# Terms by one transpose, layer 0 by pairs of blocks, and a list scheduler that knows product kinds, in a four-layer graph network on one core

## The chip, the cores and the metric

The kernel runs on one core of one Trainium2 chip. Its engines are TensorE (PE: matmuls and transposes), VectorE (DVE), ScalarE (ACT), GpSimd (POOL) and SyncE (SP, which here only issues DMAs); DMAs are also issued from ACT and POOL. The metric is device time in microseconds (us), the median of some runs. "Granted clock" is the share of full TensorE clock that the profile's rows show.

## The reference

For 16 graphs of N = 1024 nodes with D = 256 features and a symmetric 0/1 adjacency with self loops (about 3% ones), four layers are applied, each with a layer norm and relu ahead of it and its result added to x:

```python
h = relu(layernorm(x)); x = x + relu(h @ W_upd + (adj.T @ (h @ W_msg)) / deg + bias)    # layer 0
h = relu(layernorm(x)); x = x + gat1(h, adj)    # 4 heads of 64, leaky slope 0.01, then relu, + h, a norm per head
h = relu(layernorm(x)); x = x + gat2(h, adj)    # 4 heads of 64, slope 0.2, then elu
h = relu(layernorm(x)); x = x + gat3(h, adj)    # 1 head of 256, slope 0.2
# an attention: Wh = h @ W; e[i,j] = leaky(a_src.Wh[i] + a_dst.Wh[j]); softmax over the neighbours j; alpha @ Wh
```

## The kernel before, in words

The attention is used in a factored form. exp(leaky(s_i + d_j)) is exp(d_j) exp(slope s_i) times max(exp((1-slope) s_i), exp(-(1-slope) d_j)), up to a factor that the softmax drops. So for each head a row r = exp((1-slope) s_i) is spread over all 128 partitions, tt = exp(-(1-slope) d_j) is a scalar per partition, and one VectorE instruction makes a block of weights p = max(r, tt) * mask (`masked`, L1054: 128x1024 for layers 1 and 2, 128x256 for layer 3). TensorE multiplies p with the projected features, scaled by exp(d_j), whose extra column exp(d_j) gives the denominators.

The nodes lie in NB = 8 blocks of 128. For each graph:
- `load_x`, `load_adjr` (L864, adjacency columns by blocks, issued by POOL) and `mask_block` load data; `mask_block` loads a row block of the adjacency (L871), squares it to bf16 on ACT (L876) and has it transposed by a DMA (L883) into the mask.
- `norm_t` (every layer): stats on DVE (L905, L912), rstd by two POOL instructions (L917, L918), a shift on DVE (L924), the normed rows hn on ACT (L937), transposes on PE (L950) and a copy to ht on ACT (L956).
- `layer0`: each block is projected (L966), copied as fp32r to hi (L1081), the rounded part is subtracted in PSUM by a matmul with minus the identity (L1088), and the rest is copied to lo (L1097). Each of the eight gathers runs over 8 blocks, hi and lo (L1110, L1113); the last two columns of hi give the degree. ACT takes the degree (L1119), POOL inverts it (L1122, L1123), ACT scales (L1129). The update is four matmul passes (L1137) and the bias as a two-row fp32r matmul of 256 columns (L1140). DVE adds both (L1146) and adds the relu to x (L1153).
- `heads` (layers 1 and 2): `project_all` (L966 and ACT's copy L984), `terms`, then for each of four heads 8 weight blocks (L1054), each followed by a product of 32 matmuls of 64 columns of p and 65 columns of features (L1194, a stationary tile of 128x64), and an epilogue on DVE, ACT and POOL (L1213 to L1332).
- `layer3`: the same with one head, a stationary tile of 128x128 (L1363), and the store of out on SP (L1398).
- `terms` turns the source terms into rows: two groups of four transposes into rows of 4 (or 1) partitions (L1005), an exp on ACT for each group (L1010), a store to DRAM (L1018), then loads that spread a row over all partitions (L1039).

An fp32 matmul appears as two rows in the profile, an fp32r one as one.

The order of all engines' instructions is written by a list scheduler, `Plan`: `do` records each operation with its engine, a cost in us, what it reads and writes, and a priority, which is TensorE's running position in program order plus `RANK[stage][engine]` plus a slack; `SHIFT` sets off the positions of successive graphs. `emit` then always takes the operation that can start earliest by its costs, and by priority among equals. A graph's operations may begin once the first operation of layer 3 of the graph two before is done by the list, so two graphs are in flight for most of the time. A DMA has a fixed `lag` from its issue to its landing, whatever else is being moved. Tiles come from pools with the numbers of buffers in `BUFS`; the PSUM pool `mm` has four banks.

Of the kernel before, what the change touches and what calls it, by code (L numbers as in the profile page):

```python
# [26 lines left out]
SHIFT = 64.5  # L27
# [3 lines left out]
    "load": (-57, -12, 31, -4, -20),  # L31
    "setup": (-11, -73, -123, -184, -81),
    "norm0": (145, -33, -116, 157, 83),
    "split0": (-76, -27, -143, -178, -68),
    "mask": (-26, 45, 20, 88, -18),
    "gather0": (99, -7, 88, 10, 13),
    "norm1": (-71, -5, -82, -24, -28),
    "project1": (17, 39, 4, 11, 39),
    "weights1": (-57, -2, 47, -12, -4),
    "heads1": (-172, -126, -154, -187, -83),  # L40
    "last1": (-121, -247, -219, -176, -156),
    "norm2": (-199, -12, -128, -69, -50),
    "project2": (-145, -175, -221, -103, -183),
    "weights2": (-2, -8, -49, 24, 18),
    "heads2": (21, -16, -35, 64, -14),
    "last2": (74, 30, 80, 28, 44),
    "norm3": (-87, -191, -295, -306, -160),
    "project3": (131, -75, 4, -44, 2),
    "weights3": (-4, 11, 73, 105, -1),
    "last3": (-60, 20, -26, 62, -10),  # L50
# [4 lines left out]
    "mv": 4, "st": 2, "rstd": 4, "shift": 4, "tt": 3, "dg": 2, "rden": 2, "sth": 1, "mh": 2, "rsh": 2,  # L55
# [16 lines left out]
class Plan:  # L72
# [3 lines left out]

    def __init__(self):
        self.ops, self.pos, self.gate, self.stage = [], 0.0, None, None

    def do(self, eng, cost, fn, r=(), w=(), lag=0.0, slack=0.0):  # L80
# [24 lines left out]
        self.ops.append((eng, cost, lag, fn, deps, bufs, self.pos + slack + RANK[self.stage][ENGINES.index(eng)]))  # L105
# [3 lines left out]
    def emit(self):  # L109
# [6 lines left out]
        done, free, held = [None] * n, {}, {}  # L116

# [5 lines left out]
        while ready:  # L123
            best = None
            for k in ready:
                eng, cost, lag, fn, deps, bufs, prio = self.ops[k]
                at = free.get(eng, 0.0)
                for d in deps:
                    same = self.ops[d][0] == eng and not self.ops[d][2]
                    at = max(at, done[d] + (0.0 if same else self.WAIT[self.ops[d][0]]))  # L130
# [13 lines left out]
            eng, cost, lag, fn, deps, bufs, _ = self.ops[k]  # L144
# [5 lines left out]
            free[eng] = at + cost  # L150
            done[k] = at + cost + lag
# [433 lines left out]
def tile_factored(  # L585
# [88 lines left out]
    def fetch(tile, part, out_of, src):  # L674

        do("act", 0.5, lambda: nc.scalar.dma_start(out_of(tile.t), src), w=[(tile, part)], lag=2.5)
# [167 lines left out]
    def load_x(b):  # L844
# [3 lines left out]
        for k in range(0, NB, NB // 2):  # L848
# [7 lines left out]
                lag=4.5,  # L856
# [630 lines left out]
```

## Time and profile before

| | |
|---|---|
| median of 3 runs | 2854.28 us (2850.51 to 2854.32) |
| the profiled execution | 2862.98 us, of which the span is 2861.1 us |
| mean granted TensorE clock | 0.969 |
| busy: PE, PE weight loads, DVE | 2652.2, 2316.5, 2447.7 us |
| busy: ACT, POOL | 1189.9, 721.1 us |
| DMA | 285.24 MB, mean 100 GB/s |

The span runs from the first to the last instruction of one profiled execution; the rest of its time lies around it. Engines work side by side, so busy times don't add up; an engine's idle time costs something only where it lies on the chain of work that ended last. The out stores' last VectorE instruction of each graph shows the graphs' ends: the first graph ends at 425.5 us, the second at 604.6, and from then on one follows another after some 169 us up to 2634.2; the last two end at 2795.3 and 2853.1.

### The profile page before, as it was taken

To read this page: it belongs to the slowest core of one execution; us is meant where nothing else is said; L and a number is where in the kernel's file an instruction comes from. 1 tells how busy PE (TensorE), PEld (TensorE's weight loads), DVE (VectorE), ACT (ScalarE), POOL (GpSimd) and SP (SyncE) were. 2 spreads that over 40 slices of the span, in tenths; PEclk is the share of its full clock that TensorE was granted. 3 is DMA by queue.
4 is the path that set the end of the run, shared out by engine and by line. 5 is a ranking of instruction groups with operands and counts; after the bars stand their busy time and mean duration, and the time that the engine had idled before them with its cause. 6 is when DMAs were issued, how large, how long until landed. Compare 5 with 4: busy or idle time off the path is not lost.

```text
span 2861.1 us, 93412 instructions
## 1 busy us (share of the span) xinstructions
PE 2652.2 (93%) x41131; PEld 2316.5 (81%) x41131; DVE 2447.7 (86%) x5014; ACT 1189.9 (42%) x2881; POOL 721.1 (25%) x811
## 2 busy tenths in 40 slices
PE   6977998999999999999999999999999999999786
PEld 5767886888888888888888888888888888888675
DVE  2579887898998988989898998989899898989984
ACT  4342525344343534535353444535344353443222
POOL 2321311323231222313123231222323122231100
PEclk9989999999999999999999999999999999999898
DMA  9612244542524345253533624353262435424010
GB/s 236 143 38 83 51 89 125 124 115 53 163 70 108 109 106 134 53 126 93 122 109 68 150 67 115 110 122 106 68 154 69 101 109 128 112 53 106 31 42 28
DMA packets 346153, 285.24 MB, mean 100 GB/s; under 512 B 145525, under 2 KB 310778, under 8 KB 345738
## 3 DMA queue, kind: packets, MB, share of 16 engines
q1 hardware_dynamic: 209424, 209.83, 26.7%
q0 software_dynamic: 133152, 67.12, 12.9%
q8 instruction: 324, 5.31, 0.8%
q10 hardware_dynamic: 3162, 2.24, 0.3%
q14 instruction: 91, 0.75, 0.1%
HBM read 228.21 MB, written 17.37 MB: 86 GB/s over the span
## 4 chain that ended last, share of the span: by engine, by line
PE 75%; DVE 15%; DMA 3%; POOL 2%; ACT 2%; issue 2%; SPq 0%; ACTq 0%; DVEq 0%; POOLq 0%
PE acc L1194 28%; PE acc L1363 15%; PE mm L966 13%; DVE p L1054 7%; PE mm L1110 4%; PE mm L1137 4%; PE mm L1113 4%; PE mm L950 4%; DVE st L905 2%; DMA mask<-sq 1%; POOL rstd L918 1%; PE mm L1140 1%; DVE x L1332 1%; PE mm L1005 1%; PE mm L1088 1%
## 5 line engine op out<-in xcount | busy, mean ns | idle before, releaser
L1054 DVE SCALAR_TENSOR_TENSOR p<-r,tt,mask 128x1024 f32<-128x1024 f32 (+1 forms) x1536 | 1468.6, 1012 | 65.7 <-PE acc L1363 44.0
L1194 PEld LDWEIGHTS acc<-wide,p 128*64 128x64 f32 x32768 | 1005.8, 140 | 168.4 <-issue 84.8
L1194 PE MATMUL acc<-wide,p 128*64 128x65 f32 x32768 | 1061.8, 225 | 78.9 <-DVE p L1054 48.5
L966 PE MATMUL mm<-f_w,ht 128*128 128x264 f32 (+2 forms) x2048 | 532.6, 403 | 5.0 <-ACT wide L984 2.5
L1363 PE MATMUL acc<-wide,p 128*128 128x257 f32 x2048 | 474.2, 386 | 12.2 <-DVE p L1054 12.2
L1363 PEld LDWEIGHTS acc<-wide,p 128*128 128x128 f32 x2048 | 382.5, 191 | 71.7 <-issue 11.2
L966 PEld LDWEIGHTS mm<-f_w,ht 128*128 128x128 f32 x2048 | 382.6, 198 | 69.3 <-ACT ht L956 6.4
L937 ACT ACTIVATE hn<-x,shift,rstd 128x256 f32<-128x256 f32 x512 | 273.1, 595 | 149.7 <-DVE shift L924 126.5
L876 ACT ACTIVATE sq<-nat 128x1024 bf16<-128x1024 int32 x128 | 136.0, 1062 | 322.2 <-DMA mask<-sq 293.5
L1110 PE MATMUL mm<-wide,adjr 128*128 128x258 f32 x1024 | 258.9, 292 | 1.6 <-ACT f_deg L1119 1.6
L1113 PE MATMUL mm<-wide,adjr 128*128 128x256 f32 x1024 | 251.8, 285 | 2.7 <-ACT wide L1097 2.7
L950 PE MATMUL mm<-f_ident,hn 128*128 128x128 f32 x1024 | 170.7, 300 | 79.9 <-ACT hn L937 78.9
L1284 ACT ACTIVATE t<-t,mh,rsh 128x64 f32<-128x64 f32 x512 | 176.9, 430 | 160.4 <-DVE mh L1274 160.3
L984 ACT COPY wide<-mm 128x264 f32<-128x264 f32 (+1 forms) x384 | 139.7, 378 | 248.9 <-PE mm L966 247.6
L917 POOL TENSOR_SCALAR rstd<-mv 128x4 f32<-128x4 f32 x128 | 60.6, 473 | 652.7 <-DVE mv L912 630.8
L950 PEld LDWEIGHTS mm<-f_ident,hn 128*128 128x128 f32 x1024 | 123.0, 150 | 114.1 <-ACT hn L937 96.1
L1110 PEld LDWEIGHTS mm<-wide,adjr 128*128 128x128 f32 x1024 | 197.7, 193 | 8.4 <-ACT f_deg L1119 1.8
L1122 POOL TENSOR_SCALAR dg<-f_deg 128x1 f32<-128x1 f32 x128 | 54.4, 425 | 588.6 <-ACT f_deg L1119 586.8
L956 ACT COPY ht<-mm 128x512 f32<-128x512 f32 x256 | 144.9, 580 | 138.9 <-PE mm L950 138.0
L1113 PEld LDWEIGHTS mm<-wide,adjr 128*128 128x128 f32 x1024 | 196.3, 192 | 3.0 <-ACT wide L1097 2.9
L1267 POOL TENSOR_SCALAR rsh<-mh 128x8 f32<-128x8 f32 x64 | 51.5, 805 | 554.1 <-DVE mh L1262 551.9
L905 DVE BATCH_NORM_STATS2 st<-x 128x6 f32<-128x256 f32 x512 | 186.0, 415 | 3.8 <-DMA x<-in_x_dram 1.9
(100 smaller groups left out, 2390.9 us busy)
## 6 DMA issues: line engine op xcount, KB each, us to landing
r<-rd SPq DMA_DIRECT2D x144, 512.0 KB
nat<-in_adj_dram SPq DMA_DIRECT2D x128, 512.0 KB
adjr<-in_adj_dram POOLq DMA_DIRECT2D x128, 512.0 KB, 5.0
out_dram<-o SPq DMA_DIRECT2D x128, 128.0 KB
x<-in_x_dram SPq DMA_DIRECT2D x31, 512.0 KB
mask<-sq SPq DMA_TRANSPOSE x128
p<-in_L_gnn_W_dram ACTq DMA_DIRECT2D x2, 256.0 KB
x<-in_x_dram ACTq DMA_DIRECT2D x1, 512.0 KB
```

Of the source, the lines that this page charges most:

```text
L905: lambda st=st, ib=ib, k=k: nc.vector.bn_stats(st.t[:, k, :], xs.t[:, ib, :]),
L937: nc.scalar.activation(hn.t[:, k, :], xs.t[:, hf * nh + q, :], AF.Relu, bias=shift.t[:, q : q + 1], scale=rstd.t[:, q : q + 1],)
L950: nc.tensor.transpose(pt.t[:, k, c, :], hn.t[:, k, c * P : (c + 1) * P], ident)
L956: nc.scalar.copy(ht.t[:, :, i0 : i0 + 2 * P].rearrange("p c (k i) -> p k c i", k=2), pt.t)
L966: nc.tensor.matmul(ps.t[:, : hi - lo], ht.t[:, c, ib * P : (ib + 1) * P], w.t[:, c, lo:hi], start=(c == 0), stop=(c == KC - 1),)
L984: lambda ib=ib, ps=ps: nc.scalar.copy(wh.t[:, ib, :cols], ps.t[:, :cols]),
L1054: lambda: nc.vector.scalar_tensor_tensor(w.t[:, : hi - lo], r.t[:, lo:hi], tt.t[:, jb, h : h + 1], mask.t[:, jb, lo:hi], op0=ALU.max, op1= ...
L1110: nc.tensor.matmul(ps.t[:, : D + 2], a.t[:, ib, :], hi.t[:, ib, : D + 2], start=(ib == 0), stop=False)
L1113: nc.tensor.matmul(ps.t[:, :D], a.t[:, ib, :], lo.t[:, ib, :D], start=False, stop=(ib == NB - 1))
L1194: nc.tensor.matmul(ps.t[c : c + 64, g, q * E1 : (q + 1) * E1], p.t[:, i2 * 64 : (i2 + 1) * 64], xw.t[:, jb, h * E1 : (h + 1) * E1], start= ...
L1284: nc.scalar.activation(t.t[:, ib, :], t.t[:, ib, :], AF.Identity, bias=mb.t[:, 3, ib : ib + 1], scale=rs.t[:, ib : ib + 1],)
L1363: nc.tensor.matmul(ps.t[:, q, : D + 1], w.t[:, q * P : (q + 1) * P], wh.t[:, jb, : D + 1], start=(jb == 0), stop=(jb == NB - 1),)
```

## The change

- `terms`: exp is taken first, on ACT, of all eight blocks' source columns (8 x 4 or 8 x 1) into a small tile es; one transpose turns it into 32 (or 8) rows of 128; ACT copies them out, and the store to DRAM writes 32 (or 8) rows of 512 bytes.
- `layer0`, split: two blocks are projected into one PSUM bank; each of the two copies and the subtraction takes both, 512 columns.
- `layer0`, update: both blocks of a pair share a bank. The bias comes first, as one two-row matmul of 512 columns, then the eight weight passes. DVE's two operations take 512 columns. The gathers, the degree and its inverse stay by block.
- `layer3`: out is stored by pairs of blocks.
- The list: each product has a kind (c: a 64-column product of layers 1 and 2, r: fp32r, f: all others; an update begins as r and ends as f), and `EMPTY` adds a cost where the kind changes. Each large DMA has a transfer time `dma`; transfers follow one another on one clock, `moved`, and an issue is not placed earlier than some 2 us before that clock comes free. Some costs of operations are new.
- All of `RANK`, `SHIFT` and the slack of the epilogues of heads 0 to 2 have new numbers.

The core of the diff (three of the twenty rows of `RANK`; other loads get `dma` in the same way as the two shown):

```diff
-SHIFT = 64.5
+SHIFT = 59.5
...
 RANK = {
-    "norm0": (145, -33, -116, 157, 83),
+    "norm0": (-17, -86, -77, -102, -43),
...
-    "heads1": (-172, -126, -154, -187, -83),
+    "heads1": (38, 4, 67, -106, 2),
...
-    "norm3": (-87, -191, -295, -306, -160),
+    "norm3": (102, -18, -111, 50, -13),
...
+    EMPTY = {"cf": 0.12, "cr": 0.12, "fc": 0.09, "fr": 0.09, "rc": 0.09, "rf": 0.19}
+
+    AHEAD = 2.0
...
-    def do(self, eng, cost, fn, r=(), w=(), lag=0.0, slack=0.0):
+    def do(self, eng, cost, fn, r=(), w=(), lag=0.0, slack=0.0, kind="f", dma=0.0):
...
+                eng, cost, lag, fn, deps, bufs, prio, kind, dma = self.ops[k]
                 at = free.get(eng, 0.0)
+                if eng == "pe":
+                    at += self.EMPTY.get(kept + kind[0], 0.0)
+                if dma:
+                    at = max(at, moved - self.AHEAD - cost)
...
-            free[eng] = at + cost
-            done[k] = at + cost + lag
+            free[eng] = done[k] = at + cost
+            if eng == "pe":
+                kept = kind[-1]
+            if dma:
+                moved = done[k] = max(moved, done[k]) + dma
+            done[k] += lag
...
-        do("pool", 1.0, lambda: nc.gpsimd.dma_start(a.t, src), w=[a], lag=6.0)
+        do("pool", 1.0, lambda: nc.gpsimd.dma_start(a.t, src), w=[a], lag=2.0, dma=2.9)
...
-        do("sp", 0.1, lambda: nc.sync.dma_start(nat.t, adj[b, ib * P : (ib + 1) * P, :]), w=[nat], lag=4.5)
+        do("sp", 0.1, lambda: nc.sync.dma_start(nat.t, adj[b, ib * P : (ib + 1) * P, :]), w=[nat], lag=2.0, dma=2.2)
...
-    def project(ps, ht, ib, w, lo, hi):
+    def project(ps, ht, ib, w, lo, hi, k=0):
 
 
         def go():
+            out = ps.t[:, : hi - lo] if hi - lo > D else ps.t[:, k, :]
             for c in range(KC):
                 nc.tensor.matmul(
-                    ps.t[:, : hi - lo],
+                    out,
                     ht.t[:, c, ib * P : (ib + 1) * P],
                     w.t[:, c, lo:hi],
-                    start=(c == 0),
+                    start=(c == 0 and k == 0),
                     stop=(c == KC - 1),
+                    skip_group_check=k > 0,
                 )
 
         do("pe", 0.88, go, r=[(ht, ib // 2), w], w=[ps])
...
-        for g in range(2):
-            pt = buf(mm_p, "mm", [P, 4, P])
-
-            def turn(pt=pt, g=g):
-                for q in range(4):
-                    nc.tensor.transpose(pt.t[:nh, q, :], wh.t[:, 4 * g + q, scol : scol + nh], ident)
-
-            do("pe", 0.46, turn, r=[(wh, 4 * g + q) for q in range(4)], w=[pt])
-
-            def raise_r(pt=pt, g=g):
-                nc.scalar.activation(
-                    r4.t[:nh, g * 512 : (g + 1) * 512],
-                    pt.t[:nh].rearrange("p q i -> p (q i)"),
-                    AF.Exp,
-                    scale=1.0 - slope,
-                )
-
-            do("act", 0.6, raise_r, r=[pt], w=[(r4, g)])
-        do("sp", 0.1, lambda: nc.sync.dma_start(rd.t, r4.t[:nh, :]), r=[r4], w=[rd], lag=2.2)
+        m = NB * nh
+        es = buf(small, "es", [P, nh, NB])
+        do(
+            "act",
+            0.25,
+            lambda: nc.scalar.activation(
+                es.t, wh.t[:, :, scol : scol + nh].rearrange("p n h -> p h n"), AF.Exp, scale=1.0 - slope
+            ),
+            r=[(wh, ib) for ib in range(NB)],
+            w=[es],
+        )
+        pt = buf(mm_p, "mm", [P, 512])
+        do(
+            "pe",
+            0.11,
+            lambda: nc.tensor.transpose(pt.t[:m, :P], es.t.rearrange("p h n -> p (h n)"), ident),
+            r=[es],
+            w=[pt],
+        )
+        do("act", 0.25, lambda: nc.scalar.copy(r4.t[:m, :P], pt.t[:m, :P]), r=[pt], w=[r4])
+        do(
+            "sp",
+            0.1,
+            lambda: nc.sync.dma_start(rd.t.rearrange("h (n i) -> (h n) i", n=NB), r4.t[:m, :P]),
+            r=[r4],
+            w=[rd],
+            lag=2.2,
+        )
 
...
-        for ib in range(NB):
-            ps = buf(mm_p, "mm", [P, 512])
-            project(ps, ht, ib, w0, 0, D)
+        for n in range(0, NB, 2):
+            ps = buf(mm_p, "mm", [P, 2, D])
+            for k in range(2):
+                project(ps, ht, n + k, w0, 0, D, k)
+            parts = [n, n + 1]
             do(
                 "act",
-                0.27,
-                lambda ib=ib, ps=ps: nc.scalar.copy(hi.t[:, ib, :D], ps.t[:, :D]),
+                0.48,
+                lambda n=n, ps=ps: nc.scalar.copy(hi.t[:, n : n + 2, :D], ps.t),
                 r=[ps],
-                w=[(hi, ib)],
+                w=[(hi, ib) for ib in parts],
             )
             do(
                 "pe",
-                0.13,
-                lambda ib=ib, ps=ps: nc.tensor.matmul(
-                    ps.t[:, :D], minus, hi.t[:, ib, :D], start=False, stop=True, skip_group_check=True
+                0.23,
+                lambda n=n, ps=ps: nc.tensor.matmul(
+                    ps.t, minus, hi.t[:, n : n + 2, :D], start=False, stop=True, skip_group_check=True
                 ),
-                r=[(hi, ib)],
+                r=[(hi, ib) for ib in parts],
                 w=[ps],
+                kind="r",
             )
             do(
                 "act",
-                0.27,
-                lambda ib=ib, ps=ps: nc.scalar.copy(lo.t[:, ib, :D], ps.t[:, :D]),
+                0.48,
+                lambda n=n, ps=ps: nc.scalar.copy(lo.t[:, n : n + 2, :D], ps.t),
                 r=[ps],
-                w=[(lo, ib)],
-            )
-            mask_block(b, ib, mask)
+                w=[(lo, ib) for ib in parts],
+            )
+            for ib in parts:
+                mask_block(b, ib, mask)
...
-            do("pe", 1.92, gather, r=[adjr[jb], hi, lo], w=[ps])
+            do("pe", 1.9, gather, r=[adjr[jb], hi, lo], w=[ps], kind="r")
             dg = buf(small, "dg", [P, 1])
-            o = buf(work, "o", [P, D])
+            pair_of = jb % 2
+            if not pair_of:
+                o = buf(work, "o", [P, 2, D])
...
-                0.35,
-                lambda ps=ps, dg=dg, o=o: nc.scalar.activation(o.t, ps.t[:, :D], AF.Copy, scale=dg.t),
+                0.38,
+                lambda ps=ps, dg=dg, o=o, q=pair_of: nc.scalar.activation(o.t[:, q, :], ps.t[:, :D], AF.Copy, scale=dg.t),
                 r=[ps, dg],
-                w=[o],
-            )
-            pu = buf(mm_p, "mm", [P, 512])
-
-            def update(pu=pu, jb=jb):
-                for c in range(KC):
-                    nc.tensor.matmul(
-                        pu.t[:, :D], ht.t[:, c, jb * P : (jb + 1) * P], w0.t[:, c, D:], start=(c == 0), stop=False
-                    )
-                nc.tensor.matmul(pu.t[:, :D], pair.to_broadcast([2, P]), b0.t, start=False, stop=True)
-
-            do("pe", 1.0, update, r=[(ht, jb // 2), (dg, "in"), w0, b0], w=[pu])
+                w=[(o, pair_of)],
+            )
+            if not pair_of:
+                continue
+            pu = buf(mm_p, "mm", [P, 2, D])
+
+            def update(pu=pu, j0=jb - 1):
+                nc.tensor.matmul(
+                    pu.t,
+                    pair.to_broadcast([2, P]),
+                    b0.t.rearrange("k (o d) -> k o d", o=1).to_broadcast([2, 2, D]),
+                    start=True,
+                    stop=False,
+                )
+                for q in range(2):
+                    for c in range(KC):
+                        nc.tensor.matmul(
+                            pu.t[:, q, :],
+                            ht.t[:, c, (j0 + q) * P : (j0 + q + 1) * P],
+                            w0.t[:, c, D:],
+                            start=False,
+                            stop=(q == 1 and c == KC - 1),
+                        )
+
+            do("pe", 2.17, update, r=[(ht, jb // 2), (dg, "in"), w0, b0], w=[pu], kind="rf")
             do(
                 "dve",
-                0.45,
-                lambda pu=pu, o=o: nc.vector.tensor_tensor(o.t, o.t, pu.t[:, :D], op=ALU.add),
+                0.63,
+                lambda pu=pu, o=o: nc.vector.tensor_tensor(o.t, o.t, pu.t, op=ALU.add),
                 r=[pu],
                 w=[o],
             )
             do(
                 "dve",
-                0.35,
+                0.62,
                 lambda o=o, jb=jb: nc.vector.scalar_tensor_tensor(
-                    xs.t[:, jb, :], o.t, 0.0, xs.t[:, jb, :], op0=ALU.max, op1=ALU.add
+                    xs.t[:, jb - 1 : jb + 1, :], o.t, 0.0, xs.t[:, jb - 1 : jb + 1, :], op0=ALU.max, op1=ALU.add
                 ),
                 r=[o],
-                w=[(xs, jb)],
+                w=[(xs, jb - 1), (xs, jb)],
...
-                do("pe", 0.96, product, r=[p, xw], w=[ps])
+                do("pe", 0.94, product, r=[p, xw], w=[ps], kind="c")
...
-            epilogue(b, h, ps, wh, xs, 19.0 if h + 1 < H else 0.0)
+            epilogue(b, h, ps, wh, xs, 13.0 if h + 1 < H else 0.0)
...
+            o = buf(work, "o", [P, 2, D])
             for q in range(2):
-                ib = 2 * i2 + q
-                o = buf(work, "o", [P, D])
                 do(
                     "dve",
                     0.42,
-                    lambda q=q, ib=ib, ps=ps, o=o, k=k: nc.vector.scalar_tensor_tensor(
-                        o.t, ps.t[:, q, :D], rdn[:, k + q : k + q + 1], xs.t[:, ib, :], op0=ALU.mult, op1=ALU.add
+                    lambda q=q, i2=i2, ps=ps, o=o, k=k: nc.vector.scalar_tensor_tensor(
+                        o.t[:, q, :],
+                        ps.t[:, q, :D],
+                        rdn[:, k + q : k + q + 1],
+                        xs.t[:, 2 * i2 + q, :],
+                        op0=ALU.mult,
+                        op1=ALU.add,
                     ),
                     r=[ps, xs],
-                    w=[o],
+                    w=[(o, q)],
                 )
-                do(
-                    "sp",
-                    0.1,
-                    lambda ib=ib, o=o: nc.sync.dma_start(out[b, ib * P : (ib + 1) * P, :], o.t),
-                    r=[o],
-                    lag=3.0,
-                )
+            do(
+                "sp",
+                0.1,
+                lambda i2=i2, o=o: nc.sync.dma_start(
+                    out[b, i2 * 2 * P : (i2 + 1) * 2 * P, :].rearrange("(q p) d -> p q d", p=P), o.t
+                ),
+                r=[o],
+                lag=2.0,
+                dma=1.2,
+            )
```

## The prediction

> **What bounds the kernel now.** I read the page first, then the groups by line, then TensorE (PE) alone: its busy time between the second and the fourteenth graph's end, its timeline in one graph, its waits.
>
> ```profile
> span 2861.1 us, 93412 instructions
> ...
> PE 2652.2 (93%) x41131; PEld 2316.5 (81%) x41131; DVE 2447.7 (86%) x5014; ACT 1189.9 (42%) x2881; POOL 721.1 (25%) x811
> ...
> PE 75%; DVE 15%; DMA 3%; POOL 2%; ACT 2%; issue 2%; SPq 0%; ACTq 0%; DVEq 0%; POOLq 0%
> ...
> 604.00:2634.00 2030.00, 1957.16 (x30838) 1710.56 (x30834) 1828.73 (x3735) 892.45 (x2160) 548.62 (x598) 0.98 0.42 104
> ```
>
> The fourth line is the window from 604 to 2634 us, in which twelve graphs end: 169.2 us for each, with PE busy 163.1 and VectorE (DVE) 152.4. PE is idle 6 us a graph, and the chain that ends last lies 75% on it. So what is saved on PE there is saved in time, until DVE, 11 us lower, stops it.
>
> PE rows overlap (a matmul's row includes its pipeline), so I cost by the distance from start to start, in a timeline of PE:
>
> ```profile
> 1009.86 1.02 PE L1137 MATMUL mm<-f_w,ht 128*128 128x256 f32 x4
> 1010.81 0.38 PE L1140 MATMUL mm<-f_bias,f_pair 2*128 2x256 f32 x1
> 1011.12 3.02 PE L1194 MATMUL acc<-wide,p 128*64 128x65 f32 x96
> 1014.07 1.13 PE L1137 MATMUL mm<-f_w,ht 128*128 128x256 f32 x4
> ...
> 1048.65 0.60 PE L1005 MATMUL mm<-f_ident,wide 128*4 128x128 f32 x4
> 1049.08 1.03 PE L1363 MATMUL acc<-wide,p 128*128 128x257 f32 x4
> ...
> 1090.29 7.69 PE L1194 MATMUL acc<-wide,p 128*64 128x65 f32 x256
> 1097.90 1.13 PE L1137 MATMUL mm<-f_w,ht 128*128 128x256 f32 x4
> ```
>
> The update of one block with its bias takes 1011.12 - 1009.86 = 1.26 us. Four weight passes, 0.216 apart inside a run, are 0.86 of it; so the bias matmul (L1140, two rows, 256 columns) costs 0.40. A fp32r matmul of that width costs 0.118 in the gather (L1110 to L1113, start to start); the other 0.28 is change: 0.09 before it, 0.19 behind it. A 64-column product of layer 1 or 2 (32 matmuls) costs (1097.90 - 1090.29)/8, less one change at the end, 0.94. The way from such a product to any other costs 0.12 before the first other matmul and 0.10 at it (the L1137 row is 1.13 behind L1194, 1.02 behind the gather); the way back costs 0.09. Four turns of the terms cost 0.43.
>
> The one regular stall, in windows:
>
> ```profile
> 1117.00:1118.30 1.30, 1.26 (x10) 0.68 (x8) 1.30 (x8) 0.82 (x2) 0.03 (x1) 1.00 1.09 407
> 1118.30:1122.80 4.50, 0.01 (x1) 0.01 (x1) 4.20 (x19) 1.70 (x6) 3.43 (x5) 0.94 0.50 190
> 1122.80:1126.00 3.20, 3.20 (x11) 2.22 (x12) 3.20 (x15) 3.20 (x7) 2.14 (x3) 0.50 0.98 236
> 1126.00:1130.00 4.00, 4.00 (x14) 3.22 (x14) 4.00 (x8) 2.04 (x6) 2.23 (x2) 0.61 1.05 305
> ...
> PE mm L950 <- ACT hn L937: 54.0, 12, 4.5
> ```
>
> Once a graph PE waits 4.5 us for the norm of layer 3, while the other graph in flight is between its terms and its weights. The clock column shows 0.50 and 0.61 for the 7.2 us behind it: 3.2x0.50 + 4.0x0.39 = 3.2 us more. The stall costs 7.7 us.
>
> **The change part by part**, for all 16 graphs.
>
> *Terms.* Eight transposes become one, 48 times: 48 x 7 x 0.109 = 36.6 us off PE. All eight blocks must now be projected first; then exp of 32 columns on ScalarE (ACT; 0.25, as L1029), the transpose, and a copy of 128 columns (between L1119 with 0.16 and L1081 with 0.38), in place of two exps of 0.58. In the trace the last projection copy ends near 1117.8 and the rd store is issued at 1118.95; the new chain is 0.25 + 0.27 + 0.27 with three handovers, the same within 0.2. DVE's first weight waits for r until 1126, and has stats to do meanwhile; without that cover it is 0.2 x 48 = 10 us either way. I take 0. The store now leaves from 32 rows of 512 B: no row is near; between no difference and another r wait like the four there are (13.0 us in all). I take 0. SP issues one store as before.
>
> *Update and bias.* Before: 128 bias matmuls x 0.40 = 51 us, and 57 of the updates (counted in the trace) follow a 64-column product: 57 x 0.22 = 12.5. After: 64 updates; the bias of 512 columns stands first: 0.236 (twice 0.118) + 0.19 behind it = 0.43, 27 us; its entry is 0.22 for some 28 and 0.09 for 36, 9.4; half the returns to a product, no longer in the bias's 0.19, 22 x 0.09 = 2. Saved 63.5 - 38.6 = 25. What the trace lacks is the step from a 64-column product or a gather straight into the two-row tile. The Trainium skill, "TensorEngine Tiling (Array Packing)", Key Properties, says that a change of tiling mode drains the array. The rows agree for two rows and for 64 columns, and show none between fp32 and fp32r of one tile (four L966 and an L1088 take 0.98 = 0.86 + 0.118). By this rule the entry from a gather, which had cost nothing into L1137, now costs 0.09, and I have counted it. Bounds: entry nothing, 34 saved; entry 0.3 each, 15. The same rule speaks against the new list: EMPTY charges 0.09 and 0.19 for fp32 to fp32r and back, which only the two-row tile pays, and too little into other work (0.12, where the rows show 0.22). It will hold apart kinds that mix freely.
>
> *Split.* 8 passes and a 512-column subtraction per pair take what two blocks took (1.73 + 0.24). The subtractions cut into products less often: 41 entries x 0.22 and 30 returns x 0.14, halved, 6.6. I take 5 (2 to 7). ACT copies 512 columns (0.58, as L956) for 2 x 0.376, so lo of a pair is there some 1 us later than that of its first block was; products of the other graph lie over it. Without them: 64 x 1 us.
>
> *DVE.* Add and relu-add of a pair at about 0.69 each (L1214 and L1246, 512 columns) for 2 x 0.42 each: 64 x 0.31 = 20 us of busy time off, 1.2 a graph. Off the path mostly; 0.
>
> *Stores of out.* 128 of 128 KB become 64 of 256 KB, each waiting for the second o (0.48 later). Behind them on SP are x and nat loads, and nobody of PE waits for those in the middle; at the very end 0.5 us. 0.
>
> *The list.* The trace has 333 ways from products to other work and 259 ways back without a bias: 333 x 0.22 + 259 x 0.09 = 97 us. The parts above dealt with 57 and 41 of the ways out, 22 us. Of the other 75, a list that sees a cost on changes keeps more work together; but DVE makes a weight in 1.28 us and PE uses it in 0.94, so PE must leave often. Bounds: 0 and half, 37; I take a fifth, 15. Pacing DMAs moves nat, adjr, x, r and out issues on SP, ACT and POOL's queues: in the middle covered (DMA share 0.42); in the first 100 us (share 1.07 in its window, PE busy 73) from -10 to +15; 0. All ranks, SHIFT and the epilogue's slack are new: where the 7.7 us stall falls next is not in the trace. I take it as it is.
>
> Sum on PE: 36.6 + 25 + 5 + 15 = 82. In the chain of that window PE's lines sum to 84%:
>
> ```profile
> by line: PE acc L1194 32.8%; PE acc L1363 16.9%; PE mm L966 14.1%; PE mm L1110 5.0%; PE mm L1137 4.6%; PE mm L1113 4.5%; PE mm L950 4.1%; DVE p L1054 3.0%; DVE st L905 1.9%; issue 1.8%; PE mm L1140 1.5%; POOL rstd L918 1.4%; DVE x L1332 1.1
> ```
>
> So 69 us. The profiled execution took 2862.98 (2861.1 of span and 1.9 around it), 8.7 over the median of the three runs; 2863 - 69 = 2794, and against the median 2854.3 - 69 = **2785**.
>
> **Rivals.**
> 1. *The stall goes.* A better matched order gives PE work under the norm of layer 3. "TensorE: Matmul & The Clock Gate", Part 1, says that an idle window of about 3.4 us halves the clock; the windows above agree (4.5 us of idle, then 0.50), and no shorter stall here shows where it begins. By the row alone half the stall is worth half of 7.7; by the rule it is worth 2.3 + 3.2 = 5.5. Some 14 graphs x 5.5 to 7.7 = 77 to 108 more: 2677 to 2708, and about 2750 if a third of the graphs gain. For it: the list that made this order reckoned updates at 1.0 where 1.26 are taken. Against: the stall is a chain of DVE, POOL and ACT (stats, pow, hn), and less PE work leaves less to lay over it. 18%.
> 2. *DVE becomes the bound.* If its 16.8 us of idle a graph stay, a graph takes 151.2 + 16.8 = 168.0: 1.2 x 16 = 19 us, 2835. Against: of 174 us of its named waits in the window some 130 are for PE or PE's copies. 12%, 2815 to 2845.
> 3. *Slower: a second stall.* Longer runs of one kind keep PE from the other graph's norm or first products, and the idle passes the point where the clock halves. Price 7.7 a graph against 69/16 = 4.3 gained: one more such stall in over 56% of the graphs turns the sign; in all of them 16 x 3.4 = 54 slower, 2908; likeliest some 2870. 6%.
> 4. *The list does not matter and the savings fall into waits*: no change, 4%.
>
> The first reading has 60%: 2750 to 2815.
>
> **How the numbers follow.** A difference under 0.2%, some 6 us, is no change for this kernel. Faster: 60 + 18 + 12 = 90%; same 4; slower 6. The range takes in the first reading with its bounds (36.6 + 15 + 2 up to 36.6 + 34 + 7 + 37, times 0.84: 45 to 96), the nearer half of the stall's case and most of DVE's: 2715 to 2832.
>
> **What would show it.** One L1005 transpose per term and 48 in all; L1140 with 512 columns, 64 times, some 0.43 to its next start; PE busy in a middle graph near 158 for 163.1, DVE near 151; fewer ways out of L1194 than 333; the L950 wait for hn still once a graph at 4 to 5 us with a clock of 0.5 behind it. It is wrong if that wait is gone or doubled, if PE's idle in the middle grows past 10 us a graph, or if the first 425 us, which graph 0 takes now, move by over 20.

## The result, and the profile after

The changed kernel takes 2807.62 us (median of 4 runs, 2803.09 to 2812.79) against 2854.3 before: a ratio of 0.9838 [0.9817, 0.986], 47 us less. That lies within the range. The way to it is another than the forecast's.

The span and the busy times of the page:

```profile
span 2807.9 us, 92058 instructions
...
PE 2535.0 (90%) x40667; PEld 2288.6 (82%) x40667; DVE 2422.9 (86%) x4886; ACT 1158.5 (41%) x2753; POOL 652.4 (23%) x811
```

PE works 117 us less (2652.2 to 2535.0), not 82, and yet the span is only 53 us shorter (the profiled execution of before was 8.7 over its median; by medians it is 47). DVE works 25 us less.

To see where 117 us became 47, each kernel is cut at the ends of the second and the fourteenth graph, into the front, the middle (twelve graphs) and the tail. The columns of a window are: its stretch and length, busy time (and number) of PE, its weight loads, DVE, ACT and POOL, the granted clock, the DMA share, GB/s. First before:

```profile
0.00:604.60 604.60, 522.69 (x7801) 456.14 (x7803) 452.63 (x942) 238.90 (x581) 152.83 (x193) 0.95 0.48 109
604.60:2634.20 2029.60, 1956.76 (x30822) 1710.16 (x30820) 1828.34 (x3735) 892.45 (x2160) 548.62 (x598) 0.98 0.42 104
2634.20:2861.10 226.90, 172.80 (x2520) 150.17 (x2516) 166.77 (x341) 58.57 (x140) 19.66 (x20) 0.90 0.11 36
```

and after:

```profile
0.00:547.40 547.40, 477.34 (x7099) 422.58 (x7099) 422.13 (x883) 224.14 (x535) 143.04 (x191) 0.95 0.51 117
547.40:2562.20 2014.80, 1865.34 (x30490) 1694.84 (x30492) 1809.70 (x3637) 869.37 (x2062) 488.08 (x601) 0.97 0.44 105
2562.20:2807.90 245.70, 192.34 (x3086) 171.17 (x3082) 191.11 (x368) 65.03 (x158) 21.29 (x21) 0.88 0.10 34
```

Front and tail have to be taken together, because the new order does less of later graphs ahead of the second end, and more behind the fourteenth. In us:

| | PE busy | PE idle | length |
|---|---|---|---|
| middle | 1956.8 to 1865.3 (-91) | 72.8 to 149.5 (+77) | 2029.6 to 2014.8 (-15) |
| front and tail | 695.5 to 669.7 (-26) | 136.0 to 123.4 (-13) | 831.5 to 793.1 (-38) |

So the two ends grew shorter by all that PE saved there, and by some idle time as well. In the middle five sixths of the saving turned into idle time of PE: a graph takes 167.9 us for 169.1, with PE busy 155.4 for 163.1, and idle 12.5 for 6.1. The waits of PE, all of them, then the first two of DVE, in the middle of after (us in total, times, longest):

```profile
PE acc L1241 <- DVE shift L940: 108.6, 12, 9.2
PE acc L1241 <- issue: 27.8, 23, 4.2
PE acc L1410 <- DVE p L1082: 7.9, 12, 0.7
PE acc L1241 <- DVE p L1082: 4.3, 10, 0.5
```

```profile
DVE f_mx L1049 <- ACT wide L1002: 94.6, 27, 7.3
DVE rden L1260 <- PE acc L1241: 33.8, 34, 5.3
```

And DVE's first line in the middle of before:

```profile
DVE f_mx L1022 <- ACT wide L984: 55.3, 12, 4.7
```

PE's wait for hn, the regular one of before, is gone from after's middle. PE now waits 9 us once a graph for DVE, in one piece; DVE waits up to 7.3 us for a projection that PE has not yet made (wide is ACT's copy of it, f_mx the maximum that DVE takes of it for the terms). They wait for each other by turns. Before, PE's one regular wait was 4.5 us, and this one of DVE's 4.6. One of PE's waits, in its timeline (start, length, line, tiles, count, and the idle time before with what ended it):

```profile
1059.69 6.17 PE L983 MATMUL mm<-f_w,ht 128*128 128x264 f32 x27
1065.79 13.29 PE L1241 MATMUL acc<-wide,p 128*64 128x65 f32 x448
1079.01 0.28 PE L1033 MATMUL mm<-f_ident,es 128*32 128x128 f32 x1
1088.31 3.56 PE L1241 MATMUL acc<-wide,p 128*64 128x65 f32 x64 [9.03 <-DVE shift L940]
```

and DVE's timeline over the same time:

```profile
1077.40 0.69 DVE L1371 SCALAR_TENSOR_TENSOR y<-y,t 128x512 f32<-128x512 f32 x1
1078.12 0.69 DVE L1379 TENSOR_TENSOR x<-x,y 128x512 f32<-128x512 f32 x1
1078.73 1.22 DVE L1222 TENSOR_TENSOR wide<-wide 128x1024 f32<-128x1024 f32 x1
...
1082.96 0.69 DVE L1379 TENSOR_TENSOR x<-x,y 128x512 f32<-128x512 f32 x1
1083.69 1.41 DVE L921 BATCH_NORM_STATS2 st<-x 128x6 f32<-128x256 f32 x4
1085.01 0.36 DVE L928 BATCH_NORM_AGGREGATE mv<-st 128x2 f32<-128x6 f32 x4
1085.29 1.37 DVE L921 BATCH_NORM_STATS2 st<-x 128x6 f32<-128x256 f32 x4
1086.58 0.36 DVE L928 BATCH_NORM_AGGREGATE mv<-st 128x2 f32<-128x6 f32 x4
1086.88 1.28 DVE L1082 SCALAR_TENSOR_TENSOR p<-r,tt,mask 128x1024 f32<-128x1024 f32 x1
```

PE has used up 14 weights in one run of 448 matmuls, and its projections lie before that run. DVE then has 9 us without a weight in it: the end of layer 2 for one graph, the statistics of its layer 3, the scaling of features for the other. The weight that PE needs is made at 1086.88 (the wait carries the name of L940, the instruction behind it). The windows:

```profile
1079.20:1088.30 9.10, 0.09 (x1) 0.02 (x1) 8.86 (x27) 1.54 (x4) 2.67 (x4) 0.62 0.68 240
1088.30:1092.00 3.70, 3.69 (x66) 3.63 (x67) 3.70 (x5) 2.05 (x4) 2.93 (x2) 0.56 1.21 269
1092.00:1096.00 4.00, 4.00 (x116) 3.83 (x117) 4.00 (x4) 3.04 (x6) 0.00 (x0) 1.00 0.77 136
```

DVE is busy 8.86 of the 9.10 us: PE waits for an engine that is at work. The clock of 0.56 behind it costs 3.7 x 0.44 = 1.6, so by its lines the stall takes 10.7 us a graph, for 7.7 before. What it is worth in time is another question (v1_tuned below).

The single products are what they were costed at. In PE's timeline:

```profile
848.85 0.27 PE L1033 MATMUL mm<-f_ident,es 128*32 128x128 f32 x1
848.96 10.57 PE L1410 MATMUL acc<-wide,p 128*128 128x257 f32 x48
859.45 0.49 PE L1172 MATMUL mm<-f_bias,f_pair 2*128 2x512 f32 x1
859.87 1.99 PE L1181 MATMUL mm<-f_w,ht 128*128 128x256 f32 x8
...
1001.04 0.28 PE L1145 MATMUL mm<-wide,adjr 128*128 128x256 f32 x1
1001.25 0.50 PE L1172 MATMUL mm<-f_bias,f_pair 2*128 2x512 f32 x1
1001.67 1.99 PE L1181 MATMUL mm<-f_w,ht 128*128 128x256 f32 x8
```

The transpose takes 0.11 from start to start, the bias 0.42, and the way from a gather into the bias 0.21, which is 0.118 and 0.09 of change.

### The profile page after: what moved, and what is told of

Its sections match the earlier page's. It is cut to its first block, busy times and chain, and to the rows that moved or that the text cites. A ratio compares the mean times of both kernels' runs of the same rounds, so it can differ in the third digit from the quotient of the medians.

```text
span 2807.9 us, 92058 instructions
## 1 busy us (share of the span) xinstructions
PE 2535.0 (90%) x40667; PEld 2288.6 (82%) x40667; DVE 2422.9 (86%) x4886; ACT 1158.5 (41%) x2753; POOL 652.4 (23%) x811
## 5 line engine op out<-in xcount | busy, mean ns | idle before, releaser
L1241 PE MATMUL acc<-wide,p 128*64 128x65 f32 x32768 | 1052.9, 227 | 204.3 <-DVE shift L940 117.6
L983 PE MATMUL mm<-f_w,ht 128*128 128x264 f32 (+2 forms) x2048 | 481.6, 390 | 4.4 <-ACT ht L972 3.9
L1410 PEld LDWEIGHTS acc<-wide,p 128*128 128x128 f32 x2048 | 388.9, 192 | 84.2 <-DVE p L1082 13.8
L966 PE MATMUL mm<-f_ident,hn 128*128 128x128 f32 x1024 | 153.8, 291 | 26.6 <-ACT hn L953 25.1
L934 POOL TENSOR_TENSOR rstd<-rstd,f_mhalf 128x4 f32<-128x4 f32 x128 | 164.8, 1287 | 10.7
L879 POOL DMA_DIRECT2D adjr<-in_adj_dram x128 | 120.9, 944 | 164.8 <-PE mm L1145 159.1
```

The lines of the kernel that those rows point to most:

```text
L934: nc.gpsimd.tensor_tensor(rstd.t, rstd.t, mhalf[:, :nh], op=ALU.pow)
L966: nc.tensor.transpose(pt.t[:, k, c, :], hn.t[:, k, c * P : (c + 1) * P], ident)
L983: nc.tensor.matmul(out, ht.t[:, c, ib * P : (ib + 1) * P], w.t[:, c, lo:hi], start=(c == 0 and k == 0), stop=(c == KC - 1), skip_group_che ...
L1241: nc.tensor.matmul(ps.t[c : c + 64, g, q * E1 : (q + 1) * E1], p.t[:, i2 * 64 : (i2 + 1) * 64], xw.t[:, jb, h * E1 : (h + 1) * E1], start= ...
L1410: nc.tensor.matmul(ps.t[:, q, : D + 1], w.t[:, q * P : (q + 1) * P], wh.t[:, jb, : D + 1], start=(jb == 0), stop=(jb == NB - 1),)
```

## The experiments

Each kernel was run beside before; ratios are against before of the same runs. Where a kernel is compared with after, the two ratios are subtracted and taken of 2854 us; as either has an interval of about 0.002 on each side, such a difference is good to some 9 us, and a share worked out from it to 0.2 or 0.3.

### The terms' transpose earlier (e8_turn_moved)

In after the transpose stands 12.4 us behind its exp in this layer. Here the order of after is kept, and only the transpose, its copy, the rd store and the first spread are moved up to where their inputs are ready.

```diff
+        new = dict(when)
+        for k in self.turns:
+            t = when[k - 1][0] + self.ops[k - 1][1] + 0.2
+            for q, step in ((k, 0.4), (k + 1, 0.45), (k + 2, 2.4), (k + 5, 0.0)):
+                new[q] = min(new[q], (t, 0))
+                t = new[q][0] + step
```

> The changed kernel's list, but once it is made, four steps of each of the 48 terms (transpose on PE, ACT's copy, the rd store, the first spread of r) are taken out and put where their inputs are ready; all other instructions keep their order. Theory A (the 9.0 us wait of PE once a graph comes from the terms' transpose standing behind some 13 products of the other graph in PE's queue, so that r lands 12 us late): the wait falls to 0 to 5 us, PE's idle in the middle from 12.5 to 5 to 8 us a graph, granted clock in the middle back from 0.970 to 0.98 or more, time 2715 to 2760. Rival B (the wait is the norm chain of layer 3 on DVE, POOL and ACT, as in the kernel before, and r is not what is late): the wait stays at 8 to 9 us and the time within 10 us of 2808.

2828.42 us, 0.9913 [0.9895, 0.993]: 21 us slower than after (the rival had the wait right and the time too low), and the wait is still 8.5 us (102.1 us for 12 in the middle). PE is not held by a late r: r came early, and DVE, whose order is fixed, was busy with other work, 8.57 us of one such wait of 8.80. That theory fell. Why the time grew is open; PE's waits in the middle for which the profile names no cause (issue) rose from 27.8 to 46.2 us. This run cannot say whether the list put that other work there because it reckoned with a late r; v1_tuned bears on that.

### No cost on changes of kind (e1_no_kinds)

```diff
-    EMPTY = {"cf": 0.12, "cr": 0.12, "fc": 0.09, "fr": 0.09, "rc": 0.09, "rf": 0.19}
+    EMPTY = {}
```

> The changed kernel with EMPTY empty: a change of kind costs the list nothing. The ranks were chosen with the charges, so the order as a whole suits it less and the time may be anywhere from 2780 to 2950. What is tested is PE's count of ways from a 64-column product to other work, 163 in the changed kernel and 333 before. Theory A (the charges keep kinds together): 260 or more ways, and PE busy 25 to 45 us over the 2535 of the changed kernel. Rival B (ranks and pairs brought the count down): under 200 ways, PE busy within 15 us of 2535.

3038.69 us, 1.0644 [1.062, 1.0667]. Ways out of 64-column products: 245, for 163 in after and 333 in before; PE is busy 2620.5. PE's longest waits:

```profile
PE acc L1241 <- DVE p L1082: 140.0, 65, 6.2
PE mm L966 <- ACT hn L953: 110.5, 12, 25.8
PE acc L1241 <- DVE wide L1224: 65.0, 6, 10.8
```

The costs do hold kinds together (82 ways out fewer), under these ranks. But without them PE is busy 85 us more and the time is 230 us longer, more than either theory had, since the list went another way at many places, into waits of up to 25.8 us. The 85 us are not the price of the ways: 82 of them at 0.22 out and 0.09 back are some 25, and part of the rest is a lower granted clock (0.94 in the middle, for 0.97). RANK was chosen with the costs, so this is no price of the costs alone; that stays open.

### No transfer clock (e3_no_clock)

```diff
-        do("pool", 1.0, lambda: nc.gpsimd.dma_start(a.t, src), w=[a], lag=2.0, dma=2.9)
+        do("pool", 1.0, lambda: nc.gpsimd.dma_start(a.t, src), w=[a], lag=6.0)
...
-        do("sp", 0.1, lambda: nc.sync.dma_start(nat.t, adj[b, ib * P : (ib + 1) * P, :]), w=[nat], lag=2.0, dma=2.2)
+        do("sp", 0.1, lambda: nc.sync.dma_start(nat.t, adj[b, ib * P : (ib + 1) * P, :]), w=[nat], lag=4.5)
```

> The changed kernel without the clock of transfers: each DMA has its old fixed lag. Same ranks. Graph 1 ends at 547 us in the changed kernel and at 605 before. Theory A (the front's gain is the paced DMA order): the end of graph 1 goes back by 30 us or more, to 577 or later, and the rest stays within 2%. Rival B (the front's gain is the ranks' and less PE work): the end of graph 1 stays within 15 us of 547.

2937.36 us, 1.0296 [1.0269, 1.0324]. Its windows over the first 100 us and to the end of the second graph, then after's first 100 us:

```profile
0.00:100.00 100.00, 65.84 (x358) 55.88 (x359) 20.68 (x81) 43.59 (x91) 26.60 (x56) 0.97 1.12 228
0.00:604.40 604.40, 482.59 (x7099) 424.94 (x7099) 424.34 (x885) 222.46 (x532) 135.92 (x192) 0.93 0.46 106
```

```profile
0.00:100.00 100.00, 82.59 (x476) 69.57 (x478) 30.55 (x110) 51.15 (x116) 36.09 (x71) 0.98 1.09 217
```

The front holds the same 7099 matmuls as after's and ends 57 us later; 52 of these are idle time of PE (121.8 for 70.1). The DMA engines moved no more in after's first 100 us (217 GB/s for 228). PE's waits for a transfer in the front, first of e3, then of after:

```profile
PE mm L725 <- DMA p<-in_L_gnn_W_dram: 15.6, 3, 14.3
PE mm L1139 <- DMA adjr<-in_adj_dram: 9.0, 3, 4.2
```

```profile
PE mm L1142 <- DMA adjr<-in_adj_dram: 3.1, 2, 2.6
```

So 22 of the 52 us are transfers that came later for PE. Another 27 are longer waits for DVE's weights and epilogues (p and t), since the list made another order of everything. The middle was to stay within 2% and became 3.4% longer. For these ranks the clock is worth the whole gain of the front. Against before, whose ranks fitted a list without it, PE's first 100 us gained 10 us (72.73 busy to 82.59).

### Only the terms (e4_terms_only)

Before, with the new `terms` and nothing else; the list makes a new order from the old ranks.

```diff
-        for g in range(2):
-            pt = buf(mm_p, "mm", [P, 4, P])
...
+            lambda: nc.tensor.transpose(pt.t[:m, :P], es.t.rearrange("p h n -> p (h n)"), ident),
```

> The kernel before with the new terms alone: one transpose in place of eight, same ranks, same list. The list is made anew with the changed costs. Theory A (the edits on PE are worth their instructions): PE busy 30 to 45 us under 2652, time 2815 to 2840. Rival B (what the list makes of a small edit is larger than the edit): PE busy as in A, but a PE idle that differs by over 40 us from the 202 of the kernel before, and a time outside 2800 to 2850, either way.

2978.08 us, 1.0445 [1.0424, 1.0467]. PE is busy 2645.4, only 7 less, where both theories had 30 to 45 (the granted clock in the middle is 0.97, for 0.98), and idle 16.1 us a graph for 6.1. An edit that takes 37 us of transposes off PE costs 127 us when the order around it is made anew from ranks that were chosen for other operations. In the runs from x1 to y1 the order was frozen and only work was changed.

### PE's work changed in a fixed order (x1_eight_turns, x3_fewer_turns, z2_no_bias)

After, with the one transpose made eight times:

```diff
+            for _ in range(8):
+                nc.tensor.transpose(pt.t[:m, :P], es.t.rearrange("p h n -> p (h n)"), ident)
```

> The changed kernel with the terms' one transpose made eight times into the same tile, all instructions in the same order: 48 x 7 x 0.109 = 36.6 us of PE work put back where the edit took it out. Theory A (in the new order PE is the bound in only part of a graph; layer 1's transposes stand right in front of the 9.0 us wait): the time grows by 8 to 22 us, the 9.0 us wait shrinks or stays. Rival B (the prediction's step: 84% of PE work is time): it grows by 31 us or more.

2829.27 us, 0.9915 [0.9893, 0.9936]: 22 us over after, for 37 us more of PE (2572.2). A share of 0.6, and give or take 9 us the rival's 31 is just within reach. Where the wait stands the addition was free: it fell from 9.0 to 8.3 us.

Before, with six of eight transposes left out:

```diff
-                for q in range(4):
-                    nc.tensor.transpose(pt.t[:nh, q, :], wh.t[:, 4 * g + q, scol : scol + nh], ident)
+                nc.tensor.transpose(pt.t[:nh, 0, :], wh.t[:, 4 * g, scol : scol + nh], ident)
```

> The kernel before with three of each four transposes of the terms left out (the exp reads the first for all four blocks, so the rows of the other blocks are left out), all instructions in the same order: 48 x 6 x 0.109 = 31.4 us of PE work less. Theory A (also before, PE is the bound in part of a graph only: layer 1's and 2's transposes stand next to the 4.5 us wait): faster by 8 to 20 us. Rival B (the prediction's step, 84%): faster by 24 to 31 us.

2841.56 us, 0.9958 [0.9941, 0.9974]: 12 us (7 to 17) under before. By the two traces PE is busy 37 us less (2614.9), but z3 below, which leaves PE's work alone, has 2644.5, 8 under before's trace; the six transposes are the 31 that were worked out. So a share of 0.4 (0.24 to 0.54). This tests the conversion on the very kernel that it was read from, and directly against it: not 0.84.

After, with the bias matmul left out:

```diff
-                nc.tensor.matmul(
-                    pu.t,
-                    pair.to_broadcast([2, P]),
...
-                            start=False,
+                            start=(q == 0 and c == 0),
```

> The changed kernel, same order, with layer 0's bias matmul left out (the part of the computation that adds the bias): 64 x 0.43 = 27 us of PE, with the entry 33 us, about 2 us a graph. Theory A (PE does not set the middle any more): 0 to 10 us faster, PE's idle grows by 1.2 us a graph or more. Rival B (PE sets layer 0's stretch, as the prediction had it with 84%): 20 to 33 us faster.

2786.5 us, 0.9761 [0.9739, 0.9784]: 22 us under after, for 36 less on PE (2498.7). Again 0.6. That is the rival's range: PE's work still counts in after, though not in full.

### DVE's work changed in a fixed order (x2_short_stats, z1_no_beta, z3_before_no_beta)

After, with the statistics of layer 3's norm over 64 columns for 256; they lie in PE's wait:

```diff
+        ht = norm_t(xs, 64)
...
+                    lambda st=st, ib=ib, k=k: nc.vector.bn_stats(st.t[:, k, :], xs.t[:, ib, :cols]),
```

> The changed kernel, same order, with layer 3's norm statistics taken over 64 of 256 columns: this leaves out three quarters of that part of the computation. Each of 8 stats falls from 0.41 to about 0.21 us on DVE, 1.6 us a graph, all of it inside the 9.0 us wait. Theory A (PE waits there because DVE is busy with other work than weights): the wait falls to 7.2 to 7.7 us and the time by 15 to 35 us. Rival B (the wait hangs on a transfer, a POOL or an ACT step): the wait stays over 8.5 us and the time within 8 us of the changed kernel's.

2780.03 us, 0.9738 [0.9721, 0.9754]: 28 us under after, for 25.5 less on DVE (2397.4). Its waits of PE in the middle:

```profile
PE acc L1241 <- DVE shift L940: 88.6, 12, 7.5
```

20 us of the wait went (from 108.6); the other 8 are within what the difference is good to. In that place DVE's work counts about one for one.

After and before, each without layer 1's addition of beta, which lies outside the wait:

```diff
-                lambda v=v, op=op: nc.vector.tensor_tensor(t.t, t.t, row(v), op=op),
+                lambda v=v, op=op: nc.vector.tensor_tensor(t.t, t.t, row(v), op=op) if v == 1 else None,
```

> The changed kernel, same order, with the add of beta in layer 1's epilogues left out: 64 adds of 0.69 us, 44 us of DVE, 2.75 us a graph. They stand among the weights of layer 1, outside the 9.0 us wait (but for the last head's). Theory A (DVE with its own waits sets the middle, wherever its work stands): 30 to 45 us faster, DVE's idle in the middle stays at 16 to 18 us a graph. Rival B (DVE sets only the stretch of the long wait, PE the rest): 0 to 15 us faster, and DVE's idle grows to 19 us a graph or more.

> The kernel before, same order, with the add of beta left out: 44 us of DVE. Theory A (already in the kernel before DVE's work was worth as much as PE's, which the removed transposes showed at 0.4): 15 to 45 us faster. Rival B (PE bounds the kernel before, as the prediction reads its profile): 0 to 10 us faster.

After: 2774.63 us, 0.9725 [0.9702, 0.9747], 32 us under after for 43 less on DVE (2379.8): 0.75, while DVE's idle time in the middle rose from 17.1 to 18.3 us a graph. Before: 2848.17 us, 0.9977 [0.9969, 0.9986], 6.5 us for some 44: 0.15. So in before, DVE's work outside the stall cost next to nothing, as the prediction had read it, and the change made it worth some five times as much. The same waits, in the middle of z1_no_beta (DVE's), and of z2_no_bias (DVE's, then PE's over its whole span):

```profile
DVE f_mx L1049 <- ACT wide L1002: 94.6, 25, 7.3
```

```profile
DVE f_mx L1049 <- ACT wide L1002: 87.6, 25, 7.1
```

```profile
PE acc L1234 <- DVE shift L940: 117.5, 13, 9.2
```

The wait of 9 us for DVE stays whole with less of PE's work (after: 117.6 over its whole span), and DVE's wait for the projection stays whole with less of DVE's.

### Residual adds on POOL (y1_pool_adds)

After, with the adds into x of heads 0 to 2 on POOL, in the same order; meant to free DVE.

```diff
-            lambda: nc.vector.tensor_tensor(xs.t[:, :, c], xs.t[:, :, c], t.t, op=ALU.add),
+            lambda: (nc.gpsimd if h + 1 < H else nc.vector).tensor_tensor(xs.t[:, :, c], xs.t[:, :, c], t.t, op=ALU.add),
```

> The changed kernel, same order on all engines, with the residual adds of heads 0 to 2 in layers 1 and 2 (96 adds of 128x512, 0.69 us each, 66 us of DVE) issued on POOL at the same places. Theory A (PE waits where DVE has other work than weights, so DVE's work is worth about its time there): the 9.0 us wait falls to 8.1 to 8.5 us (one such add stands in front of it), and the time falls by 10 to 45 us. Rival B (POOL's add is so slow, or slows DVE beside it, that x or the next weights come late): between no change and 25 us slower, with POOL over 1.6 us an add or the weights' rows longer than 1.28 us.

2850.35 us, 0.9983 [0.9974, 0.9992]: 41 us over after, outside both forecasts; PE's long wait rose to 9.5 us. Some of its groups (busy us, mean ns of one, idle before it with what ended that):

```profile
L1344 DVE TENSOR_TENSOR t<-t,f_rows 128x512 f32<-128x512 f32 x128 | 98.5, 770 | 8.2 <-ACT t L1331 6.0
L1379 POOL TENSOR_TENSOR x<-x,y 128x512 f32<-128x512 f32 x48 | 90.3, 1881 | 457.2 <-DVE y L1371 457.2
L1261 DVE TENSOR_TENSOR t<-acc,rden 128x512 f32<-128x512 f32 x128 | 88.5, 691 | 63.7 <-POOL x L1352 60.3
L1352 POOL TENSOR_TENSOR x<-x,t 128x512 f32<-128x512 f32 x48 | 76.2, 1588 | 134.6 <-DVE t L1344 133.8 <-DVE mh L1321 0.8
```

An add takes 1.6 to 1.9 us on POOL for 0.69 on DVE, DVE is slowed beside it (L1344 takes 770 ns in the mean, for 688), and it now waits 60 us for POOL. Of 66 us taken from DVE (96 x 0.69) only 19 showed in its busy time.

### A new order without the long wait (v1_tuned)

After's operations, the transpose without a charge on its kind and taken early, and RANK, SHIFT and the slack chosen anew.

```diff
-SHIFT = 59.5
+SHIFT = 53.6761
...
+            slack=-400.0,
+            kind="t",
...
-            epilogue(b, h, ps, wh, xs, 13.0 if h + 1 < H else 0.0)
+            epilogue(b, h, ps, wh, xs, 35.113 if h + 1 < H else 0.0)
```

> The changed kernel's products; the terms' transpose is free of the charge for a change of kind and goes first among equals, and RANK, SHIFT and the slack are chosen anew for that, so that no wait of PE over some 3 us is left in the middle. Theory A (the order, not the products, keeps the savings back): PE's idle in the middle 12.5 to under 9 us a graph, granted clock in the middle 0.98 or more, 2740 to 2795. Rival B (PE and DVE take turns as bound whatever the order, and idle that goes in one place comes back in others): idle stays over 11 us a graph, 2795 to 2850.

2812.45 us, 0.9856 [0.9837, 0.9875]: not told apart from after. PE's waits in its middle:

```profile
PE acc L1243 <- DVE p L1084: 83.9, 82, 2.2
PE acc L1243 <- issue: 24.8, 20, 2.7
```

No wait is longer than 2.7 us and the clock in the middle is 0.99, but PE is still idle 10.5 us a graph (between the two forecasts), now in small pieces for weights. DVE's wait for the projection is there as before (91.4 us in the middle), and its busy and idle time of a graph is 150.9 + 15.8 = 166.7. So an order without the long wait is no faster. As all ranks differ, this doesn't price the wait alone; the reading that it is only the form in which one order shows that DVE doesn't deliver fits, and is not shown beyond that.

## Why the prediction was right or wrong

The total was right, in part by luck: PE saved more than forecast (117 us for 82), and what is saved on PE was worth less (0.40 for 0.84). The two errors point in opposite directions; their product, 47 us, is two thirds of the 69 forecast.

- **Terms, and update with bias: right.** Start to start, the terms' transposes fell by 38 us (36.6 was worked out), update and bias by 25 to 27 (25). The entry from a gather costs 0.09, as had been counted though the trace of before had no such step.
- **Split: right.** The subtractions' own rows fell by 14 us, but 11 of these belong to the projections: where a subtraction follows one, the last projection row starts only 0.03 us ahead of it and the subtraction's row takes 0.31, together the 0.216 + 0.118 of the two. Before has 76 such places, after 16. That leaves 3 us, and with the 27 ways out of products that went here, at 0.12, some 6 (5).
- **The list: too small.** What remains is some 48 of the 117, where a fifth of the ways that were left, 15, had been taken and 37 was the upper bound. Ways out that are not at updates or subtractions went from 235 to 132, ways back from 259 to 120: at 0.22 and 0.09 that is 35 us. The rest has not been placed. (The 259 that the prediction calls ways back without a bias also leaves out the 30 behind subtractions.) That the costs in EMPTY bring fewer ways out is seen in e1; how much of it they bring is not.
- **The step that failed: "what is saved on PE there is saved in time", at 0.84.** On 117 us it gave 47: 0.40. The chain's share of lines says where the last chain ran, not what a saving is worth. x3 shows some 0.4 on before itself. The prediction named the limit ("until DVE, 11 us lower, stops it") and then did not use it: 7.7 us a graph off PE was to meet DVE's 152.4 + 16.8.
- **Rival 2 describes the middle.** It said 151.2 + 16.8 = 168.0 us a graph. Measured: 150.8 + 17.1 = 167.9. It was doubted because most of DVE's waits are for PE, and so were to shrink as PE does less. They still are for PE or its copies, some 150 of 182 us in the middle, and did not shrink; that they stay because PE's waits are for DVE in turn is what z1 and z2 suggest. That the sum agrees to 0.1 us is luck: DVE's idle time is not fixed (18.3 in z1, 15.8 in v1). Its total of 2835 was off because it knew nothing of the ends. DVE alone is not the bound either: after, PE's work is worth 0.6 (x1, z2) and DVE's 0.75 to 1.1 (z1, x2), shares that are too rough to rank the two.
- **The stall "as it is": wrong.** The wait for hn went, and another of twice the length, 9.0 us, stands in its place: not for a chain of DVE, POOL and ACT in a norm, but for a weight that DVE makes after 9 us of other work (x2). Rival 3, a second stall, foresaw longer waits and a slower kernel; the kernel became faster with one long wait, and v1 without it is no faster.
- **The ends: not foreseen.** Pacing the DMAs was taken as 0 between -10 and +15; PE's first 100 us gained 10. With the PE work saved there (26 us, in full) the ends gave 38 of the profiled 53. All three signs that the prediction listed against itself came: its wait is gone, PE's idle is over 10 us a graph, and the first graph ends at 352.5 for 425.5, for the most part because less of the next graphs is done ahead of it (PE busy 294.8 us until then, for 356.8).

What stays open: what held before, where neither PE's work (0.4) nor DVE's (0.15) was worth its time; the worth of the kinds' costs and of the transfer clock apart from the ranks that were chosen with them (e1 and e3 change both), and whether an order exists in which PE and DVE stop waiting for each other by turns.

## What to carry to other kernels

Where a second engine is close behind the first (here 152 of 163 us a graph), price a saving on the first also by what the second's busy and idle times leave: if its idle time is waits for the first's products in a loop, it may not shrink, and its busy plus idle time is then a second forecast. It is a rough one. It gave the middle of after (168.0 for 167.9) and came near z1's (148.1 + 17.1 = 165.2 for 166.4), but it misses y1's (149.6 + 17.1 = 166.7 for 171.0), where new waits came. A chain's share is no worth; freezing the order and adding or leaving out a known piece of work on one engine measures the worth directly. And don't judge one part of a change under a list whose ranks were chosen for the other: e4 lost 127 us to an edit that only takes work away.

## What the runs showed of the hardware

- The granted clock behind 9.0 us of idle PE is 0.56 for 3.7 us and then 1.00; before, behind 4.5 us of idle, it was 0.50 for 3.2 us and 0.61 for 4.0. A wait of twice the length cost no more clock (1.6 us for 3.2).
- A 128x512 add on POOL took 1.59 and 1.88 us in the mean, for 0.69 on DVE. DVE's rows that overlap such an add grew: 13 of the 32 copies of 16 columns (L1224) took 1.26 us, the other 19 0.17; 13 of the 128 rows of L1344 (128x512) took 1.49 us, the other 115 0.69. But the 13 rows of L1222 (128x1024) that overlap one took 1.22 us, as those that don't.
- An fp32r product next to an fp32 one on the same 128x128 tile costs nothing above its own pass: the last fp32 row of a projection and the subtraction behind it take 0.03 + 0.31 us before (0.216 + 0.118 = 0.33), and a layer 3 product and a gather behind it the same after. Nor does a transpose with 32 or 8 stationary columns between full tiles (0.11). The two-row tile (0.09 in, 0.19 out) and the 64-column tile (0.12 + 0.10 out, 0.09 back) do cost time.
